# A gated recurrence on one core: the order of the twelve products of a step, and of one VectorE update

## The chip, the cores and the metric

The kernel runs on one core of a Trainium2 chip. The metric is the time of one execution on the device in microseconds (us), the median of several runs. A profile comes from one execution of its own. In it PE is TensorE (matmuls), PEld is TensorE's loading of the stationary operand, DVE is VectorE, ACT is ScalarE, POOL is GpSimd and SP is SyncE. L188 is line 188 of the kernel.

## The reference

x is (8 batches, 512 steps, 512 features), float32. Each step uses the state h of the step before:

```python
def step(h, x_t):
    fused = jax.nn.sigmoid(jnp.concatenate([x_t, h], axis=-1) @ w_W + w_b)
    hidden_state, output_state = jnp.split(fused, 2, axis=-1)
    memory_state = x_t @ wx_W + wx_b + hidden_state * (h @ wh_W + wh_b)
    h_new = output_state * h + (1.0 - output_state) * jnp.tanh(memory_state)
    return (h_new, h_new)
_, hs = jax.lax.scan(step, h0, xT)
return x + jnp.swapaxes(hs, 0, 1)
```

Below, r is the first half of the fused gate (hidden_state), z the second (output_state), and hh is h @ wh_W + wh_b. Every step needs three products of h (8 x 512) with 512 x 512 weights, for r, z and hh, and they can't start before the step before has given h. The products of x don't depend on h.

## The kernel before, in words

**Layout.** The 512 units of h are cut in four chunks k of 128. Chunks 0 and 1 are half A (`hT[0]`, in the profile hTA), chunks 2 and 3 half B (`hT[1]`, hTB). A chunk is the stationary operand of a product: 128 partitions x 32 columns, where the 32 columns are four steps x 8 batches, and only the columns of the present step are not zero. So the four steps of a group (`GS = 4`) add up in the same PSUM banks, and only the eight rows of the present step count (`rows`).

**Products.** The outputs are spread over the four 32-partition quadrants j of PSUM, so that each product consists of four matmuls of 32 output partitions, one in each column group of TensorE. There are three banks: A holds hh, z and r of half A (192 columns), B holds r and hh of half B (128 columns), C holds z of half B (64 columns). With four chunks each, a step has twelve products, A0 to A3, B0 to B3 and C0 to C3, each of four matmuls; a float32 matmul appears in the profile as two records. The order is written out by hand in `ORDER` (L27), and the first step has one of its own, `FIRST`. The loop at L338 issues them; the quadrant it begins with moves on:

```python
for j in range(NQ):
    j = (j + turn[0]) % NQ
    to = ps[bank] if i or bank != "A" else xps[0][:, XP["A"]]
    mm(to[32 * j : 32 * j + 32, :], hs, wh(bank, k, j))
```

Behind the twelve products of a step the loop takes seven quadrant matmuls of the x side (`take(later, 7)`, `turn[0] += 7`), 192 columns each, for a pair of groups that comes later (`products`). The x side ends some steps before the last one. Each bank exists twice; ScalarE copies the x side's part into the idle set in advance (`spread`).

**From the banks to the new h.** A product A0 needs chunk 0 of the new h, A1 chunk 1, A2 and A3 those of half B. The order of instructions on every engine is the order of the program. For each half (hf) VectorE transposes r (`turn_r`, L374, tr), hh (`turn_h`, L390, md1) and z (`turn_z`, L374, tz) out of PSUM; r and hh of half B come from bank B, its z from bank C. ScalarE takes the sigmoid of r (md0) and of z (hd0). `memory(hf, q)` is a scan on VectorE for chunk q of the half (L358, m) and a tanh of it on ScalarE. `update(hf, q)` is a scan on VectorE (L358, hTA or hTB) that makes the new h of the chunk, and the weight load of the next step's first product with that chunk waits for it. In the loop:

```python
turn_r(0)
turn_h(0)
turn_z(0)
memory(0, 0)
memory(0, 1)
turn_r(1)
turn_h(1)
update(0, 0)
turn_z(1)
tc.add_manual_dep(update(0, 1), r_done[1].name, SYNC)
```

and then memory(1, 0), memory(1, 1), update(1, 0) and update(1, 1). Behind these VectorE has one transposition of the x side (L256), in some steps an addition (L475) and two tiny memsets (L505); ScalarE copies the new h and prepares banks; GpSimd adds x to h for the output (L507), which SyncE's queue stores every 16 steps.

Of the kernel before, what the change touches and what calls it, by code (L numbers as in the profile page):

```python
# [23 lines left out]
LAST = 4  # L24
SYNC = mybir.DependencyInfo(mybir.DependencyClass.Sync, mybir.DependencyReason.DATA)

ORDER = "A0 B0 A1 A2 A3 B1 B2 B3 C0 C1 C2 C3"  # L27

FIRST = "A0 x A1 x A2 x A3 B0 B1 B2 B3 C0 C1 C2 C3"

# [11 lines left out]
def tile_cond_rnn_residual(  # L42
# [172 lines left out]
    def act(key, out_, in_, func, **kw):  # L215
        inst = nc.scalar.activation(out_, in_, func, **kw).ins  # L216
        if key in written:
            tc.declare_no_dep(inst, written[key], reason="ordered through VectorE")
        written[key] = inst
        return inst  # L220
# [108 lines left out]
    for i in range(T):  # L329
# [7 lines left out]

        for n in (ORDER if i else FIRST).split():  # L338
            if n == "x":
# [16 lines left out]
        def scan(c_, out_, d0, d1):  # L356

            return nc.vector.tensor_tensor_scan(  # L358
                *[t_[:, :, c_].rearrange("p n c s -> p (n c s)") for t_ in (out_, d0, d1)],
                0.0,  # L360
                ALU.mult,
                ALU.add,
            ).ins
# [8 lines left out]
        def turned(n, hf):  # L372
            t_ = work.tile([P, 2, 32], F32, tag=f"t{n}{hf}", name=f"t{n}{hf}_{i}")
            inst = nc.vector.transpose(t_.rearrange("p c n -> p (c n)"), raw[n][hf]).ins  # L374
            return t_[:, :, rows], inst
# [4 lines left out]
        def turn_r(hf):  # L380
            tr, _ = turned("r", hf)
            r_done[hf] = act(
                ("r", hf, g % 2, s),
                md0[hf][g % 2][:, rows, :, 1].rearrange("p n c -> p c n"),
                tr,
                AF.Sigmoid,
            )

        def turn_h(hf):
            inst = nc.vector.transpose(  # L390
                md1[hf][g % 2][:, :, :, 0].rearrange("p n c -> p c n"), raw["h"][hf]
            ).ins
            h_done[hf] = inst
            if hf == 0 and i + 1 - NH in pool_done:
                tc.add_manual_dep(inst, pool_done[i + 1 - NH].name, SYNC)

        def turn_z(hf):
            tz, _ = turned("z", hf)
            if hf == 0:
                inst = nc.vector.memset(idle[:, IDLE - 1 :], 0.0).ins  # L400
                tc.add_manual_dep(inst, h_done[0].name, SYNC)
            act(
                ("zc", hf, i % 2),
                hd0[hf][i % 2][:, :, :, 2].rearrange("p n c -> p c n"),
                tz,
                AF.Sigmoid,
                scale=-1.0,
            )
# [6 lines left out]
        def memory(hf, q):  # L415

            c_ = slice(q, q + 1)
            scan(c_, ms[hf], md0[hf][g % 2][:, rows], md1[hf][g % 2][:, rows])
            act(("n", hf, q, i % NH), state(hf, i, 1)[:, :, c_], ms[hf][:, :, c_, 1], AF.Tanh)

        def update(hf, q):
            s1 = (i + 1) % GS
            new = hT[hf][(i + 1) % NH][:, B * s1 : B * s1 + B]
            return scan(slice(q, q + 1), new, hd0[hf][i % 2], hT[hf][i % NH][:, rows])
# [4 lines left out]
        memory(0, 0)  # L429
        memory(0, 1)  # L430
        turn_r(1)
        turn_h(1)
        update(0, 0)
        turn_z(1)
        tc.add_manual_dep(update(0, 1), r_done[1].name, SYNC)
        if i == 0:
# [169 lines left out]
```

## Time and profile before

| | |
|---|---|
| median of 3 runs | 1672.12 us (1671.9 to 1674.32) |
| profiled execution | 1670.8 us, its span from the first to the last instruction |
| mean granted TensorE clock | 0.999 |
| busy: PE, PEld, DVE, ACT, POOL | 99%, 98%, 65%, 62%, 18% |
| matmul records: 192, 128, 64 columns | 329, 273, 219 ns (mean of one, with hTA) |

The profiled execution lies 1.3 us below the median of the runs. Each row of the page's groups gives the line, the engine, the operation, what it writes and reads, the shapes and the count; then the busy time of the group, the mean length of one, and the idle time of the engine just before them with what ended it. Matmuls are pipelined, several run at a time, and their ends are modelled, so a busy PE is not a PE at its peak. A row of a timeline gives the start, the length, the engine, the line, the operation and the count of records merged in it, and in brackets the idle time before it with what ended it.

### The profile page before, as it was taken

The numbers are of one execution on the slowest core, as the hardware profiler recorded it, in microseconds if no ns is written. First come the engines' busy times: TensorE is split into PE (matmuls) and PEld (weight loads), VectorE is DVE, ScalarE is ACT, GpSimd is POOL, SyncE is SP. The second block draws the span as 40 slices with busy tenths as digits, with TensorE's granted clock in tenths as the row PEclk, the third lists the DMA queues.
The fourth block names the chain that finished last, engine by engine and source line by source line (L and its number), as shares of the span: only waits on it lengthen the run. The fifth ranks groups of instructions, "written<-read, shape, count | busy, mean of one in ns | idle before, by whom it ended". The sixth has DMA issues, their size and how long they took to land.

```text
span 1670.8 us, 129875 instructions
## 1 busy us (share of the span) xinstructions
PE 1659.0 (99%) x56238; PEld 1637.5 (98%) x56238; DVE 1090.5 (65%) x9387; ACT 1029.9 (62%) x5822; POOL 301.9 (18%) x1281
## 2 busy tenths in 40 slices
PE   8999999999999999999999999999999999999998
PEld 5999999999999999999999999999999999999997
DVE  6666666666666666666666666666666666666666
ACT  3666666666666666666666666666666666666665
POOL 1111111111111111111111111111111111111111
PEclk9999999999999999999999999999999999999999
DMA  4000000000000000000000000000000000000000
GB/s 179 17 5 17 18 18 17 17 6 17 17 18 18 5 17 18 17 17 5 18 17 17 18 11 12 18 17 17 18 5 17 17 18 17 5 17 12 11 12 10
DMA packets 11525, 31.40 MB, mean 19 GB/s; under 512 B 1220, under 2 KB 1732, under 8 KB 10824
## 3 DMA queue, kind: packets, MB, share of 16 engines
q1 hardware_dynamic: 10800, 22.94, 4.0%
q8 instruction: 440, 7.21, 1.8%
q14 instruction: 133, 1.09, 0.2%
q10 hardware_dynamic: 152, 0.16, 0.0%
HBM read 14.70 MB, written 8.39 MB: 14 GB/s over the span
## 4 chain that ended last, share of the span: by engine, by line
PE 98%; DVE 1%; DMA 0%; issue 0%; ACT 0%
PE A L188 44%; PE B L188 23%; PE xp L188 20%; PE C L188 12%; DMA rows<-in_bias_dram 0%; DVE tr L374 0%; DVE m L358 0%; DVE tz L374 0%; DVE md1B L390 0%; DVE md1A L390 0%; DVE hTA L358 0%; DVE bias L203 0%; ACT hTB L216 0%; ACT xp L224 0%; DVE rows L120 0%
## 5 line engine op out<-in xcount | busy, mean ns | idle before, releaser
L188 PE MATMUL A<-wa,hTA 128*32 128x192 f32 x8176 | 638.2, 329 | 2.3 <-DVE hTA L358 2.3
L188 PE MATMUL B<-wb,hTA 128*32 128x128 f32 x8192 | 573.8, 273 | 0.0
L188 PE MATMUL A<-wa,hTB 128*32 128x192 f32 x8176 | 507.4, 326 | 0.5 <-DVE hTB L358 0.5
L188 PEld LDWEIGHTS B<-wb,hTA 128*32 128x32 f32 x8192 | 471.2, 122 | 1.4 <-issue 0.2
L374 DVE STREAM_TRANSPOSE tr<-A 128x64 f32<-128x64 f32 x511 | 127.7, 250 | 463.5 <-PE A L188 463.5
L188 PE MATMUL B<-wb,hTB 128*32 128x128 f32 x8192 | 398.9, 273 | 0.0
L188 PEld LDWEIGHTS A<-wa,hTA 128*32 128x32 f32 x8176 | 385.4, 123 | 7.6 <-DVE hTA L358 4.0
L188 PEld LDWEIGHTS A<-wa,hTB 128*32 128x32 f32 x8176 | 372.9, 122 | 2.7 <-DVE hTB L358 0.8
L216 ACT ACTIVATE md0A<-tr 128x16 f32<-128x16 f32 x512 | 112.3, 219 | 421.0 <-DVE tr L374 421.0
L507 POOL TENSOR_TENSOR ot<-xin,hTB 128x16 f32<-128x16 f32 x503 | 125.9, 250 | 1324.5 <-DVE hTB L358 1314.0
L188 PEld LDWEIGHTS B<-wb,hTB 128*32 128x32 f32 x8192 | 321.5, 122 | 0.1
L188 PE MATMUL C<-wb,hTA 128*32 128x64 f32 x8192 | 289.4, 219 | 0.0
L188 PE MATMUL C<-wb,hTB 128*32 128x64 f32 x8192 | 288.9, 220 | 0.2 <-issue 0.2
L188 PEld LDWEIGHTS C<-wb,hTA 128*32 128x32 f32 x8192 | 266.7, 122 | 0.0
L188 PE MATMUL xp<-tw,sx 128*32 128x192 f32 x2976 | 237.2, 326 | 0.1
L188 PEld LDWEIGHTS C<-wb,hTB 128*32 128x32 f32 x8192 | 229.2, 123 | 0.4 <-issue 0.4
L358 DVE TENSOR_TENSOR_SCAN hTB<-hd0B,hTB 128x24 f32<-128x24 f32 x1024 | 157.8, 195 | 101.0 <-ACT hTB L216 99.8
L358 DVE TENSOR_TENSOR_SCAN hTA<-hd0A,hTA 128x24 f32<-128x24 f32 x1024 | 191.0, 187 | 0.0
L188 PE MATMUL xp<-wx,xin 128*32 128x192 f32 (+1 forms) x2048 | 182.4, 331 | 0.7 <-issue 0.5
L216 ACT ACTIVATE hd0B<-tz 128x16 f32<-128x16 f32 x512 | 115.2, 225 | 93.7 <-DVE tz L374 93.7
L216 ACT ACTIVATE hTB<-hTB 128x16 f32<-128x16 f32 x512 | 120.5, 235 | 79.8 <-DVE hTB L358 72.3
L216 ACT ACTIVATE hTB<-m 128x8 f32<-128x8 f32 x1024 | 160.6, 206 | 0.0
(92 smaller groups left out, 2489.6 us busy)
## 6 DMA issues: line engine op xcount, KB each, us to landing
xin<-in_x_dram SPq DMA_DIRECT2D x31, 256.0 KB, 3.5
out_dram<-ot SPq DMA_DIRECT2D x31, 256.0 KB, 2.2
wx<-in_wx_dram SPq DMA_DIRECT2D x4, 768.0 KB, 7.1
wa<-in_wa_dram SPq DMA_DIRECT2D x4, 384.0 KB, 8.9
wb<-in_wb_dram SPq DMA_DIRECT2D x1, 1152.0 KB
wb<-in_wb_dram SPq DMA_DIRECT2D x1, 384.0 KB, 11.1
out_dram<-ot SPq DMA_DIRECT2D x1, 192.0 KB, 3.9
head<-in_xh_dram ACTq DMA_DIRECT2D x1, 144.0 KB, 5.0
```

The source lines that it names most:

```text
L188: nc.tensor.matmul(out_, lhsT, rhs, start=start, stop=False, skip_group_check=True)
L216: inst = nc.scalar.activation(out_, in_, func, **kw).ins
L358: return nc.vector.tensor_tensor_scan(*[t_[:, :, c_].rearrange("p n c s -> p (n c s)") for t_ in (out_, d0, d1)], 0.0, ALU.mult, ALU.add,).ins
L374: inst = nc.vector.transpose(t_.rearrange("p c n -> p (c n)"), raw[n][hf]).ins
L507: return engine.tensor_tensor(ot[:, t, 2 * hf : 2 * hf + 2, :].rearrange("p c n -> p n c"), x_of(c, slice(2 * hf, 2 * hf + 2), t, 1).rearr ...
```

## The change

The order of products is changed so that all four products of bank B (r and hh of half B) stand behind the four of bank A. On VectorE the first update of half A goes ahead of the transposition of hh of half B.

```diff
-ORDER = "A0 B0 A1 A2 A3 B1 B2 B3 C0 C1 C2 C3"
+ORDER = "A0 A1 A2 A3 B0 B1 B2 B3 C0 C1 C2 C3"
...
         memory(0, 0)
         memory(0, 1)
         turn_r(1)
+        update(0, 0)
         turn_h(1)
-        update(0, 0)
         turn_z(1)
         tc.add_manual_dep(update(0, 1), r_done[1].name, SYNC)
```

The first step keeps its own order of products.

## The prediction

> **What bounds the kernel now.** I read the page first, then the waits, then VectorE's, ScalarE's and TensorE's timelines of single steps in the middle of the run, and last the steps at its very end, which have no products of x.
>
> ```profile
> span 1670.8 us, 129875 instructions
> ...
> PE 1659.0 (99%) x56238; PEld 1637.5 (98%) x56238; DVE 1090.5 (65%) x9387; ACT 1029.9 (62%) x5822; POOL 301.9 (18%) x1281
> ...
> PEclk9999999999999999999999999999999999999999
> ...
> L188 PE MATMUL A<-wa,hTA 128*32 128x192 f32 x8176 | 638.2, 329 | 2.3 <-DVE hTA L358 2.3
> ...
> L188 PE MATMUL B<-wb,hTA 128*32 128x128 f32 x8192 | 573.8, 273 | 0.0
> ...
> L188 PE MATMUL C<-wb,hTA 128*32 128x64 f32 x8192 | 289.4, 219 | 0.0
> ...
> L216 ACT ACTIVATE hTB<-m 128x8 f32<-128x8 f32 x1024 | 160.6, 206 | 0.0
> ...
> PEld A L188 <- DVE hTA L358: 4.0, 11, 0.4
> ```
>
> TensorE looks full; the longest wait for h that it is charged with is 4.0 us in all (last row, from the waits). But a matmul of 273 or 329 ns is one of four that run side by side in the four column groups (the product's quadrant j), so a gap in one group is covered by the other three and appears in no idle column. I therefore take the time apart by group. The end of the run shows the groups in lockstep (TensorE's timeline; start, length, records):
>
> ```profile
> 1658.77 0.83 PE L188 MATMUL A<-wa,hTB 128*32 128x192 f32 x16
> 1659.42 0.40 PE L188 MATMUL B<-wb,hTA 128*32 128x128 f32 x8
> 1659.64 0.62 PE L188 MATMUL B<-wb,hTB 128*32 128x128 f32 x16
> 1660.08 0.41 PE L188 MATMUL C<-wb,hTA 128*32 128x64 f32 x16
> 1660.30 0.41 PE L188 MATMUL C<-wb,hTB 128*32 128x64 f32 x16
> ```
>
> A product is two records in each group. Sixteen A records are four per group: (1659.42 - 1658.77)/4 = 0.1625 us each. B: 24 records, six per group, (1660.08 - 1659.42)/6 = 0.11. C: (1660.30 - 1660.08)/4 = 0.055. A group owes each step eight of each kind: 8 x (0.1625 + 0.11 + 0.055) = 2.62 us. The x side adds seven quadrant products of 192 columns: three groups get 4 records (a long turn, 2.62 + 0.65 = 3.27), one gets 2 (a short turn, 2.62 + 0.325 = 2.945). The mean is 3.19. The start j rotates by seven, so the group that has just had its short turn is first in the next step's list: it leads, and it is the one that meets every wait.
>
> ```profile
> 73.58 0.25 DVE L374 STREAM_TRANSPOSE tr<-A 128x64 f32<-128x64 f32 x1 [0.94 <-PE A L188]
> 1618.98 0.25 DVE L374 STREAM_TRANSPOSE tr<-A 128x64 f32<-128x64 f32 x1 [0.95 <-PE A L188]
> 1631.82 0.25 DVE L374 STREAM_TRANSPOSE tr<-A 128x64 f32<-128x64 f32 x1 [0.73 <-PE A L188]
> 1656.59 0.25 DVE L374 STREAM_TRANSPOSE tr<-A 128x64 f32<-128x64 f32 x1 [0.94 <-PE A L188]
> 1659.67 0.25 DVE L374 STREAM_TRANSPOSE tr<-A 128x64 f32<-128x64 f32 x1 [0.94 <-PE A L188]
> ```
>
> Steps 16 to 496 take (1618.98 - 73.58)/480 = 3.220 us each, a few long ones included; the undisturbed four up to 1631.82 take 3.21. That is 0.02 above the 3.19 of pure streaming. Without x (last two rows) a step still takes 3.08: the loop of h through the other engines is nearly as long as the streaming. One step of that loop, on VectorE, with two tanh rows of ScalarE and two weight loads of TensorE:
>
> ```profile
> 802.27 0.25 DVE L374 STREAM_TRANSPOSE tr<-A 128x64 f32<-128x64 f32 x1 [1.02 <-PE A L188]
> 802.44 0.21 DVE L390 STREAM_TRANSPOSE md1A<-A 128x64 f32<-128x64 f32 x1
> 802.58 0.21 DVE L374 STREAM_TRANSPOSE tz<-A 128x64 f32<-128x64 f32 x1
> 802.81 0.28 DVE L358 TENSOR_TENSOR_SCAN m<-md0A,md1A 128x16 f32<-128x16 f32 x2
> 803.00 0.23 DVE L374 STREAM_TRANSPOSE tr<-B 128x64 f32<-128x64 f32 x1
> 803.15 0.21 DVE L390 STREAM_TRANSPOSE md1B<-B 128x64 f32<-128x64 f32 x1
> 803.28 0.20 DVE L358 TENSOR_TENSOR_SCAN hTA<-hd0A,hTA 128x24 f32<-128x24 f32 x1
> 803.40 0.22 DVE L374 STREAM_TRANSPOSE tz<-C 128x64 f32<-128x64 f32 x1
> 803.55 0.17 DVE L358 TENSOR_TENSOR_SCAN hTA<-hd0A,hTA 128x24 f32<-128x24 f32 x1
> 803.64 0.25 DVE L358 TENSOR_TENSOR_SCAN m<-md0B,md1B 128x16 f32<-128x16 f32 x2
> 804.09 0.31 DVE L358 TENSOR_TENSOR_SCAN hTB<-hd0B,hTB 128x24 f32<-128x24 f32 x2 [0.20 <-ACT hTB L216]
> ...
> 803.03 0.32 ACT L216 ACTIVATE hTA<-m 128x8 f32<-128x8 f32 x2
> ...
> 803.84 0.32 ACT L216 ACTIVATE hTB<-m 128x8 f32<-128x8 f32 x2
> ...
> 803.54 0.31 PEld L188 LDWEIGHTS A<-wa,hTA 128*32 128x32 f32 x8
> ...
> 804.35 0.36 PEld L188 LDWEIGHTS A<-wa,hTB 128*32 128x32 f32 x8
> ```
>
> Both first loads wait for VectorE: A0's comes at 803.54, 0.06 after the scan that ends at 803.48; A2's at 804.35, 0.06 after the first hTB scan (804.09 + 0.20, the length of the hTA scan of the same shape). Whether that wait costs anything depends on the leading group having other matmuls left. The step before shows both sides of that:
>
> ```profile
> 800.27 0.37 PE L188 MATMUL A<-wa,hTA 128*32 128x192 f32 x1
> ...
> 800.45 0.49 PE L188 MATMUL A<-wa,hTA 128*32 128x192 f32 x6
> 800.64 0.27 PE L188 MATMUL B<-wb,hTA 128*32 128x128 f32 x1
> 800.71 0.33 PE L188 MATMUL A<-wa,hTA 128*32 128x192 f32 x1
> ```
>
> The leader's late A0 record at 800.27 lasts 0.37 instead of 0.33: a matmul whose load came late pays 0.04 on top of the wait. And A0's eighth record starts at 800.71, after the leader's first B0 record at 800.64, which stands behind it in the program: groups run ahead of each other, and a late load holds its own group.
>
> **One formula.** The group that is last in step n issues the last matmul of each bank, has its short turn, and leads step n+1. If nothing holds it, 2.945 us lie between the same product of the two steps. If the loop from that product in step n, as the last group runs it, to h being loaded for it in step n+1 takes L, the group stalls d = L - 2.945. Each group leads once in four steps, so a step takes 3.19 + d/4 while only the leader stalls.
>
> Before, for A0. From A0's start the last group streams A0 0.325, B0 0.22, A1 to A3 0.975, of which the last record lasts 0.326 instead of 0.1625: 1.68. Then about 0.04 to VectorE (in the rows ahead the last A record of lockstep ends 1658.77 + 0.83 = 1659.60 and tr starts at 1659.67, 0.07, which I keep as the upper bound, with 0 as the lower; I take 0.04, with which this sum meets the measured step), 803.28 - 802.27 = 1.01 to the scan, its 0.20, 0.06 to the load, and the 0.04 of a late load: L = 3.03, d = 0.085, step 3.21. Measured: 3.21. For A2 in the same way: 0.65 of A2 and A3, again with the longer last record, 0.815; 0.04; 804.09 - 802.27 = 1.82; 0.20 + 0.06 + 0.04: 2.975, d = 0.03, less than the 0.085 that the leader has lost at A0 already. So before, the leader stalls at A0 and nowhere else.
>
> **The change part by part.** No instruction is added, and no DMA or queue entry of SP or POOL moves. Two things move.
>
> (1) B0 (eight records, two per group, 0.22 us) goes from between A0 and A1 to behind A3. Between A0 and the end of bank A there is 0.22 less, so A0's L falls to 2.81, below 2.945: A0's stall goes. That gives back 0.085/4 = 0.021 per step. VectorE's tr of half A follows bank A's end as before; but the ends of banks B and C now lie 0.22 later behind it. What each meets on VectorE:
> - tr<-B stands 0.73 behind tr<-A. Bank B's last record starts 0.1625 + 7 x 0.11 = 0.93 behind A's last, lasts 0.273 against 0.326: it ends 0.88 after A's end, and tr<-B now has to wait, some 0.15 us. Queued behind it are the second half's transposes and both updates of half A.
> - tz<-C stands 1.13 behind tr<-A. Bank C's last record starts 0.1625 + 8 x 0.11 + 7 x 0.055 = 1.43 behind A's last (eight B records, then eight of C), lasts 0.219: it ends 1.32 after A's. So tz<-C starts at about 1.32 and is 0.19 late; through B alone it would be 0.15 late. C decides. Behind it on VectorE stand update(0,1), both m scans and the hTB scans; ScalarE's sigmoid of it stands ahead of the two tanh.
>
> L for A2 is then: A2, A3 0.65, B 0.88, seven C records 0.385, the last 0.219, 2.13; 0.04 to VectorE; 804.09 - 803.40 = 0.69 from tz to the scan; 0.20 + 0.06 + 0.04: 3.16. d = 0.215, which costs 0.054 per step. By B alone it would be 0.65 + 0.77 + 0.273 + 0.04 + (804.09 - 803.00) + 0.30 = 3.12, d = 0.175, 0.044.
>
> (2) update(0,0) moves ahead of turn_h(1). The three items between tr<-B and tz<-C stay the same three, 803.40 - 803.00 = 0.40 in sum, so tz and what follows it do not move for it. The scan wants to start 0.15 behind tr<-B; its tanh, the first of the two at 803.03, ends at 803.24 by the 206 ns of the page's row, and the scan of before follows at 803.28. With tr<-B 0.15 late it starts at 803.30, so the wait of (1) just covers it. Without that cover it would wait for ScalarE about 0.13 and carry md1B and tz<-C with it. A0's h comes no later than now, and A0 isn't what is late. Worth: nothing.
>
> **Sum.** A step goes from 3.21 to 3.19 + 0.054, 3.244: +0.034. Products of x are issued in steps 5 to 500 (62 pairs of groups with 56 quadrant products each, seven a step), 496 of them: +16.9 us. The 11 steps without x go from 3.08 to 3.21 (the loop alone; for A0 above, L is 3.03 where these steps take 3.08, so I add 0.05 to 3.16): +0.13 each, +1.4. The profiled execution goes from 1670.8 to 1689.1; the median of the runs lies 1.3 above it: **1690.4**.
>
> Bounds: with 0.07 instead of 0.04 into VectorE d grows by 0.03, +3.7 us, 1694; with 0 it shrinks by 0.04, 1685. If C does not decide but B, 0.0225 x 496 + 1 = +12, 1684.
>
> **The rivals.**
> *All four groups held.* If the late load stops every group and not only the leader, the leader's lead is lost each step and the step is as long as a long turn, 3.27: +0.06 x 496 + 1.4 = +31, **1703**. Against it stand the rows of 800.27 to 800.71, where the groups run apart. For it: the leader of one step is the second group of the next, a long turn of 3.27 later against a step of 3.244, so with d = 0.215 the second group comes to A2 only 0.03 after the leader is let go, and a slightly longer L holds it too. The Trainium skill (TensorE: Matmul & The Clock Gate, Part 3, "The mechanism") says that matmuls start and end strictly in program order; that would be this rival, and the trace disagrees with it. Chance 0.14.
>
> *Faster: A0's stall goes and A2's does not come.* 0.021 x 496 = -10.4: **1662**. It needs L for A2 at 2.945 or less, 0.2 below my sum: tz<-C would have to start where it does now with C's end 0.22 later. For it speaks only that bank A really ends earlier after A0, and that the next load has cover to spare at A0. Against it, A2's load is already the one 0.06 behind its scan, and the change takes 0.22 of cover from in front of it. Chance 0.05.
>
> *Nothing that can be told.* The two stalls cancel (d at A2 about 0.085, L about 3.03): 1672. It needs 0.13 less than my sum, below the bound through B (3.12). Chance 0.05. A change of 0.2% (3.3 us) is about what a measurement of this kernel can tell from none.
>
> **How the numbers follow.** My case, 1682 to 1697, has 0.73; all groups held 0.14; 0.03 for something slower yet; faster 0.05; same 0.05. The range 1682 to 1704 takes in my bounds and the first rival. Slower by over 0.2%: 0.90.
>
> **What would show it.** Right: the idle time before VectorE's tr<-B, now none, is about 0.15 us a step and put down to PE B; tz<-C waits for PE C a few hundredths; the first hTB scan starts about 2.0 behind tr<-A instead of 1.82; A0's loads no longer sit directly behind their scan while the first A<-hTB record of a step comes late with the others' matmuls running on; the last steps are 3.2 apart. Wrong: tr<-B without a wait, first hTB scan still 1.82 behind tr<-A, or the end of the run at 3.08 or less; or steps of 3.27, with the four groups in lockstep in the middle of the run.

## The result, and the profile after

The changed kernel takes 1691.05 us (median of 4 runs, 1690.09 to 1692.14) against 1672.3 us of the kernel before in the same comparison: 1.011 of its time, 95% interval 1.0098 to 1.0122. The profiled execution went from 1670.8 to 1687.9 us. The forecast was 1690.4.

The page and the waits of the changed kernel:

```profile
span 1687.9 us, 129875 instructions
...
PE 1677.6 (99%) x56238; PEld 1607.4 (95%) x56238; DVE 1166.3 (69%) x9387; ACT 1071.6 (63%) x5822; POOL 301.1 (18%) x1281
...
L188 PE MATMUL A<-wa,hTA 128*32 128x192 f32 x8176 | 566.5, 326 | 0.2
L188 PE MATMUL A<-wa,hTB 128*32 128x192 f32 x8176 | 471.6, 329 | 0.9 <-DVE hTB L358 0.7
...
L188 PEld LDWEIGHTS A<-wa,hTB 128*32 128x32 f32 x8176 | 285.6, 123 | 50.4 <-DVE hTB L358 5.6
```

The same instructions, and TensorE as full as before. Two small things tell of the change: the mean A record with hTA went from 329 to 326 ns, the one with hTB from 326 to 329, so the matmuls that pay for a late load are now those of half B; and the weight loads of A<-hTB now have 50.4 us of idle time in front of them (2.7 before). The columns of waits still name next to nothing.

One step in the middle on VectorE, to be read beside the step from 802.27 to 805.46 in the prediction:

```profile
818.18 0.25 DVE L374 STREAM_TRANSPOSE tr<-A 128x64 f32<-128x64 f32 x1 [0.79 <-PE A L188]
...
818.71 0.28 DVE L358 TENSOR_TENSOR_SCAN m<-md0A,md1A 128x16 f32<-128x16 f32 x2
819.05 0.25 DVE L374 STREAM_TRANSPOSE tr<-B 128x64 f32<-128x64 f32 x1
819.23 0.17 DVE L358 TENSOR_TENSOR_SCAN hTA<-hd0A,hTA 128x24 f32<-128x24 f32 x1
819.31 0.22 DVE L390 STREAM_TRANSPOSE md1B<-B 128x64 f32<-128x64 f32 x1
819.50 0.25 DVE L374 STREAM_TRANSPOSE tz<-C 128x64 f32<-128x64 f32 x1
819.67 0.17 DVE L358 TENSOR_TENSOR_SCAN hTA<-hd0A,hTA 128x24 f32<-128x24 f32 x1
819.76 0.25 DVE L358 TENSOR_TENSOR_SCAN m<-md0B,md1B 128x16 f32<-128x16 f32 x2
820.20 0.31 DVE L358 TENSOR_TENSOR_SCAN hTB<-hd0B,hTB 128x24 f32<-128x24 f32 x2 [0.19 <-ACT hTB L216]
```

Counted from tr<-A, tr<-B comes at 0.87 (0.73 before), the first hTA scan at 1.05 (1.01), tz<-C at 1.32 (1.13), the first hTB scan at 2.02 (1.82). Half B's new h is 0.2 us later behind bank A's end. On TensorE in that step (matmuls, then weight loads), and last the weight load of A0 in the kernel before that belongs to the matmul of 800.27 in the prediction:

```profile
819.60 0.33 PE L188 MATMUL A<-wa,hTA 128*32 128x192 f32 x1
819.71 0.38 PE L188 MATMUL xp<-wx,xin 128*32 128x192 f32 x3
819.76 0.97 PE L188 MATMUL A<-wa,hTA 128*32 128x192 f32 x15
820.46 0.92 PE L188 MATMUL A<-wa,hTB 128*32 128x192 f32 x16
...
819.45 0.12 PEld L188 LDWEIGHTS A<-wa,hTA 128*32 128x32 f32 x1
...
820.46 0.56 PEld L188 LDWEIGHTS A<-wa,hTB 128*32 128x32 f32 x16
...
800.27 0.31 PEld L188 LDWEIGHTS A<-wa,hTA 128*32 128x32 f32 x7
```

A0's first load still comes directly behind its scan (819.23 + 0.17 = 819.40, the load at 819.45), but its matmul follows only at 819.60, at full pace (0.33 long), while before both began at 800.27 and the matmul took 0.37: the leader's earlier records now last longer than the wait for h, and the stall at A0 is gone. A2's first load comes at 820.46, 0.06 behind its scan (820.20 + 0.20), and its matmul starts with it. The leader's four A0 and A1 records had their turn from 819.60 to 820.25 (4 x 0.1625), so it stood still for about 0.2.

The records can be given to their column groups by the order of the program and the streaming times. In 275 of the 281 steps from 200 to 480 exactly one group comes late to A2; it loses 0.23 there on average, 0.19 of it waiting and 0.04 in its first record. A quarter of 0.23 on 3.19 gives 3.247, the measured step (3.246, below).

The three x records from 819.71 belong to the other groups and stand ahead of the A0 record of 819.60 in the program, so the groups still run apart. The Trainium skill (TensorE: Matmul & The Clock Gate, Part 3, "The mechanism") has matmuls start strictly in program order; these rows don't show that for matmuls in different column groups. They are records, though, and a float32 matmul has two: the first records of those x matmuls start at 819.54 to 819.60, so whole matmuls keep the program's order here. In the kernel before they don't: when the first C2 record starts, six records of C0 and C1 are still to start in 227 of the 280 steps from 200 to 479, and with whole matmuls in order it would be three at most.

How long a step is (tr<-A of steps 16, 496, 500, 503 and 511):

```profile
73.83 0.25 DVE L374 STREAM_TRANSPOSE tr<-A 128x64 f32<-128x64 f32 x1 [0.79 <-PE A L188]
...
1634.25 0.25 DVE L374 STREAM_TRANSPOSE tr<-A 128x64 f32<-128x64 f32 x1 [0.80 <-PE A L188]
...
1647.24 0.25 DVE L374 STREAM_TRANSPOSE tr<-A 128x64 f32<-128x64 f32 x1 [0.56 <-PE A L188]
...
1656.93 0.25 DVE L374 STREAM_TRANSPOSE tr<-A 128x64 f32<-128x64 f32 x1 [0.77 <-PE A L188]
...
1682.73 0.25 DVE L374 STREAM_TRANSPOSE tr<-A 128x64 f32<-128x64 f32 x1 [0.88 <-PE A L188]
```

Undisturbed, (1647.24 - 1634.25)/4 = 3.25 us (3.246 from the unrounded starts) against 3.210; without products of x, (1682.73 - 1656.93)/8 = 3.225 against 3.079. Over all of steps 16 to 496 the mean is (1634.25 - 73.83)/480 = 3.251 against 3.220: 0.031 x 496 + 0.146 x 11 = 17.0 us, and the profiled execution grew by 17.1.

### The profile page after: what moved, and what is told of

The parts are those of the page before. It is cut to its first block, busy times and chain, and to the rows that moved or that the text cites. A ratio compares the mean times of both kernels' runs of the same rounds, so it can differ in the third digit from the quotient of the medians.

```text
span 1687.9 us, 129875 instructions
## 1 busy us (share of the span) xinstructions
PE 1677.6 (99%) x56238; PEld 1607.4 (95%) x56238; DVE 1166.3 (69%) x9387; ACT 1071.6 (63%) x5822; POOL 301.1 (18%) x1281
## 4 chain that ended last, share of the span: by engine, by line
PE 98%; DMA 1%; DVE 0%; issue 0%; ACT 0%; SPq 0%
PE A L188 40%; PE B L188 26%; PE xp L188 19%; PE C L188 13%; DMA wb<-in_wb_dram 1%; DMA wx<-in_wx_dram 0%; ACT hTB L216 0%; ACT xp L224 0%; DVE hTB L358 0%; DVE tz L374 0%; SPq L125 0%; DVE tr L374 0%; DVE md1B L390 0%; DVE hTA L358 0%; ACT hd0B L216 0%
## 5 line engine op out<-in xcount | busy, mean ns | idle before, releaser
L188 PE MATMUL A<-wa,hTA 128*32 128x192 f32 x8176 | 566.5, 326 | 0.2
L188 PE MATMUL B<-wb,hTA 128*32 128x128 f32 x8192 | 343.1, 273 | 0.7 <-DMA wb<-in_wb_dram 0.7
L188 PE MATMUL B<-wb,hTB 128*32 128x128 f32 x8192 | 343.3, 273 | 0.1
L188 PEld LDWEIGHTS A<-wa,hTB 128*32 128x32 f32 x8176 | 285.6, 123 | 50.4 <-DVE hTB L358 5.6
L188 PEld LDWEIGHTS B<-wb,hTA 128*32 128x32 f32 x8192 | 292.6, 122 | 1.9 <-DMA wb<-in_wb_dram 1.1
L188 PEld LDWEIGHTS B<-wb,hTB 128*32 128x32 f32 x8192 | 265.7, 122 | 0.3 <-DMA wb<-in_wb_dram 0.3
L188 PE MATMUL C<-wb,hTB 128*32 128x64 f32 x8192 | 234.0, 219 | 0.4 <-issue 0.4
L188 PE MATMUL C<-wb,hTA 128*32 128x64 f32 x8192 | 234.0, 219 | 0.0
L188 PEld LDWEIGHTS C<-wb,hTA 128*32 128x32 f32 x8192 | 211.6, 122 | 0.0
L216 ACT ACTIVATE hTA<-m 128x8 f32<-128x8 f32 x1024 | 161.2, 207 | 0.0
```

The lines of the kernel that those rows point to most:

```text
L188: nc.tensor.matmul(out_, lhsT, rhs, start=start, stop=False, skip_group_check=True)
```

## The experiments

The theory is that of the prediction: a step costs 3.19 us of streaming plus a quarter of what the leading column group waits for h. That a step is never less than the loop of h itself is added here; the prediction's sum has it only for the steps without x. The rivals are that the moved update is at fault, that the order of products as such is (cover for another product, program order, streaming), and that every group, or none, pays for a late h. Times are compared with runs of the kernel before on the same chip, 1671.5 us for the first four experiments, 1672.7 for the next three, 1671.6 for the last two.

**The order of products alone.**

```diff
-ORDER = "A0 B0 A1 A2 A3 B1 B2 B3 C0 C1 C2 C3"
+ORDER = "A0 A1 A2 A3 B0 B1 B2 B3 C0 C1 C2 C3"
```

> The new order of products with the old order on VectorE. Theory (the leading column group stalls at A2 because banks B and C end later behind bank A; the move of the update is covered by the wait for bank B and worth nothing): as with the whole change, 1690 us within 3, the first hTB scan about 2.03 us behind tr<-A, the last steps 3.2 us apart. Rival (the moved update delays the transpose of hh of half B and is what costs): 1672 us, hTB scan at 1.82.

Measured: 1691.24 us, ratio 1.0115 (1.0101 to 1.0129). VectorE in one step, tr<-A at 820.18:

```profile
821.05 0.25 DVE L374 STREAM_TRANSPOSE tr<-B 128x64 f32<-128x64 f32 x1
821.22 0.23 DVE L390 STREAM_TRANSPOSE md1B<-B 128x64 f32<-128x64 f32 x1
821.35 0.17 DVE L358 TENSOR_TENSOR_SCAN hTA<-hd0A,hTA 128x24 f32<-128x24 f32 x1
821.50 0.25 DVE L374 STREAM_TRANSPOSE tz<-C 128x64 f32<-128x64 f32 x1
...
822.20 0.31 DVE L358 TENSOR_TENSOR_SCAN hTB<-hd0B,hTB 128x24 f32<-128x24 f32 x2 [0.19 <-ACT hTB L216]
```

tz<-C and the hTB scan lie where they lie in the whole change, 1.32 and 2.02 behind tr<-A, with the old order of the update. The first hTA scan stands at 1.17 instead of 1.05, so the moved update does give A0 its h 0.12 sooner; but nothing waits for it, since even here the first A0 matmul starts 0.05 behind its load (median of 280 steps). The order of products explains the whole loss; the update's move adds nothing to it. The rival of the update falls.

**The update alone.**

```diff
         turn_r(1)
+        update(0, 0)
         turn_h(1)
-        update(0, 0)
```

> The old order of products with update(0,0) in front of turn_h(1). Theory: tr<-B doesn't wait for bank B here, so the update stands behind its tanh for about 0.13 us and makes tz<-C about 0.10 late; L for A2 is 2.975 + 0.10 = 3.075, d = 0.13 instead of the 0.085 lost at A0, + 0.011 us a step: 1677 us, the hTA scan still 1.01 behind tr<-A. Rival 1 (the move gives A0 its h 0.13 earlier and is worth something): 1662 us. Rival 2 (the move is what costs in the whole change): 1691 us.

Measured: 1678.71 us, ratio 1.0041 (1.0028 to 1.0053). One step, tr<-A at 813.83:

```profile
814.56 0.22 DVE L374 STREAM_TRANSPOSE tr<-B 128x64 f32<-128x64 f32 x1
814.83 0.21 DVE L358 TENSOR_TENSOR_SCAN hTA<-hd0A,hTA 128x24 f32<-128x24 f32 x1
814.96 0.24 DVE L390 STREAM_TRANSPOSE md1B<-B 128x64 f32<-128x64 f32 x1
815.11 0.21 DVE L374 STREAM_TRANSPOSE tz<-C 128x64 f32<-128x64 f32 x1
```

The hTA scan stands at 1.00, no sooner than before: it waits for its tanh, and md1B and tz<-C wait with it on the engine that works in order. tz<-C is at 1.28 instead of 1.13, 0.15 late where I had expected 0.10: md1B follows the scan by 0.13. So the move is worth nothing with the new order and costs 0.4% with the old one. The cover that the prediction named for it, the wait for bank B, is real.

**B0 one place later, still ahead of A2.**

```diff
-ORDER = "A0 B0 A1 A2 A3 B1 B2 B3 C0 C1 C2 C3"
+ORDER = "A0 A1 B0 A2 A3 B1 B2 B3 C0 C1 C2 C3"
```

> B0 behind A1 instead of behind A0, everything else as before. Theory (what counts is that one B product stands in front of A2 as cover and one fewer behind A3; not where it stands ahead of A2): 1672 us, no change, step 3.21. Rival (B0 is cover for the second update of half A, so A1 directly behind A0 stalls): the load of A1 moves with its scan, the time lies between 1675 and 1691 us.

Measured: 1671.03 us, ratio 0.9998 (0.9989 to 1.0006). In the trace A1's first load moves from 1.75 to 1.50 behind tr<-A, to just behind its scan, and still costs nothing. What counts is on which side of A2 and A3 B0 stands.

**Two products of bank B ahead of A's end.**

```diff
-ORDER = "A0 B0 A1 A2 A3 B1 B2 B3 C0 C1 C2 C3"
+ORDER = "A0 B0 B1 A1 A2 A3 B2 B3 C0 C1 C2 C3"
```

> Two B products (B0 and B1) ahead of A's end, old VectorE order: the move in the other direction. Theory: L for A0 grows by the 0.22 us of B1 from 3.03 to 3.25, d = 0.305, 3.19 + d/4 = 3.266; but a step can't be shorter than the loop itself, 3.25 + 0.05 = 3.30 us, so all four groups are held: + 0.09 x 496 + 0.22 x 11 = 1719 us, and the last steps are 3.30 us apart like all the others. Rival 1 (only the leader ever stalls): + 0.056 x 496 + 2.4 = 1702 us. Rival 2 (the more of B stands in front of A2, the more cover, and the faster): 1655 us.

Measured: 1714.37 us, ratio 1.0258 (1.0242 to 1.0273). Steps 496, 500, 503 and 511 begin here:

```profile
1657.43 0.25 DVE L374 STREAM_TRANSPOSE tr<-A 128x64 f32<-128x64 f32 x1 [1.05 <-PE A L188]
...
1670.62 0.25 DVE L374 STREAM_TRANSPOSE tr<-A 128x64 f32<-128x64 f32 x1 [0.81 <-PE A L188]
...
1680.51 0.25 DVE L374 STREAM_TRANSPOSE tr<-A 128x64 f32<-128x64 f32 x1 [1.05 <-PE A L188]
...
1706.87 0.25 DVE L374 STREAM_TRANSPOSE tr<-A 128x64 f32<-128x64 f32 x1 [1.16 <-PE A L188]
```

(1670.62 - 1657.43)/4 = 3.298 us with products of x, (1706.87 - 1680.51)/8 = 3.295 without: the step is the loop, and the products of x come free. All four groups wait, by the records given to them: the leader 0.29 ahead of A0, and in each group the second A0 record comes 0.03 to 0.04 late. The expected 1719 was 5 us too much. More cover in front of A2 doesn't help; it lengthens the loop through bank A and A0.

**C0 in B0's old place, with the whole change.**

```diff
-ORDER = "A0 A1 A2 A3 B0 B1 B2 B3 C0 C1 C2 C3"
+ORDER = "A0 C0 A1 A2 A3 B0 B1 B2 B3 C1 C2 C3"
```

> The whole change, but with C0 where B0 stood: A0 C0 A1 A2 A3 B0 B1 B2 B3 C1 C2 C3. Bank C ends 0.055 x 2 = 0.11 us sooner behind bank A, bank B as late as in the whole change; A0's loop is 2.92, below 2.945. Theory (in the whole change C's end decides, and B's end lies close behind it): tz<-C starts 0.04 sooner behind tr<-A and no longer waits for the bank, L falls from 3.16 to the 3.12 of bank B, step about 3.233: 1684 us. Rival (C's end alone is what costs): L falls by the full 0.11 to 3.05, d = 0.105, 1675 us. Rival (B's end alone is what costs): 1691 us, no change against the whole change.

Measured: 1684.98 us, ratio 1.0072 (1.0058 to 1.0086). One step, tr<-A at 815.22:

```profile
816.09 0.25 DVE L374 STREAM_TRANSPOSE tr<-B 128x64 f32<-128x64 f32 x1
...
816.35 0.23 DVE L390 STREAM_TRANSPOSE md1B<-B 128x64 f32<-128x64 f32 x1
816.50 0.21 DVE L374 STREAM_TRANSPOSE tz<-C 128x64 f32<-128x64 f32 x1
...
817.19 0.31 DVE L358 TENSOR_TENSOR_SCAN hTB<-hd0B,hTB 128x24 f32<-128x24 f32 x2 [0.19 <-ACT hTB L216]
```

tr<-B still waits for bank B, 0.87 behind tr<-A; tz<-C follows md1B at once and comes at 1.28 instead of 1.32, the hTB scan at 1.97 instead of 2.02. So in the whole change bank C's end is what decides, bank B's lies close behind, as the prediction had it.

**h of half B later, no product moved: two tiny memsets.**

```diff
         turn_z(1)
+        for n in range(2):
+            nc.vector.memset(idle[:, n : n + 1], 0.0)
         tc.add_manual_dep(update(0, 1), r_done[1].name, SYNC)
```

> The kernel before with two memsets of one column on VectorE between turn_z(1) and update(0,1): the new h of half B comes about 0.15 us later in each step, and no product is moved. Theory (only the leading column group pays, and it leads once in four steps): L for A2 2.975 + 0.15 = 3.125, d = 0.18, step 3.235; with the end of the run 1685 us, and hTB scan at 1.96 behind tr<-A. Rival 1 (every step pays the delay in full): + 0.15 x 507 = 1747 us. Rival 2 (a step is the longer of streaming and loop, and the loop of 3.08 + 0.10 still lies below 3.21): 1672 us.

Measured: 1673.2 us, ratio 1.0 (0.9992 to 1.0009). The dose was not what I took it for. The trace has the hTB scan at 1.86 and not at 1.96 behind tr<-A: two memsets of one column delay what is behind them by 0.05 us, not by 0.15. (All these kernels have one such memset already, behind half A's tz, which the list of VectorE's work above leaves out.) With 0.05 the theory's L is 3.025, d = 0.08, below the 0.085 lost at A0: no cost. The run only excludes that each step pays in full (0.05 x 507 = 25 us); the time doesn't tell the theory from rival 2. The trace shows where the delay went: the first A2 matmul starts 0.105 behind its load in the kernel before and 0.055 here (medians of 280 steps in the middle of the run), so it ate half of the cover that was there.

**One such memset in the changed kernel.**

```diff
         turn_z(1)
+        nc.vector.memset(idle[:, :1], 0.0)
```

> The whole change with one such memset behind turn_z(1): h of half B about 0.06 us later. The changed kernel's last steps, the loop alone, take 3.225 us, its steps with products of x 3.246. Theory: the loop becomes 3.225 + 0.06 = 3.285, longer than 3.19 + d/4 = 3.26, so all four groups are now held and the step is the loop: + 0.04 x 496 + 0.06 x 11 = 1711 us, all steps 3.285 apart. Rival 1 (only the leader pays): + 0.015 x 496 + 1 = 1699 us. Rival 2 (each step pays in full already): + 0.06 x 507 = 1721 us.

Measured: 1702.7 us, ratio 1.018 (1.0166 to 1.0194). One step, tr<-A at 824.86:

```profile
826.18 0.25 DVE L374 STREAM_TRANSPOSE tz<-C 128x64 f32<-128x64 f32 x1
826.36 0.20 DVE L358 TENSOR_TENSOR_SCAN hTA<-hd0A,hTA 128x24 f32<-128x24 f32 x1
826.39 0.06 DVE L435 MEMSET idle<- 128x1 f32 x1
...
826.92 0.31 DVE L358 TENSOR_TENSOR_SCAN hTB<-hd0B,hTB 128x24 f32<-128x24 f32 x2 [0.19 <-ACT hTB L216]
```

The delay is 0.045 and not 0.06 (hTB scan at 2.06 behind tr<-A), so the loop is 3.27 and the time less than expected. Steps with and without x take the same 3.27 us, more than the leader's formula gives (3.26). But 3.27 is also the prediction's long turn, so this run doesn't show whether the loop or the streaming of the long turns sets the step, nor that all four groups are held: in this step the leader comes to A2 0.2 late (827.19) and the other three on time 0.04 to 0.06 behind it. Much the same delay that cost nothing in the kernel before costs 11.6 us here (1702.7 against 1691.1; the kernel before took 1672.7 and 1672.3 beside them).

**Longer memsets in the kernel before.** Since the small dose had missed, two larger ones, with a tile of 96 or 192 columns:

```diff
         turn_z(1)
+        nc.vector.memset(pad, 0.0)
```

> The kernel before with a memset of 96 columns on VectorE between turn_z(1) and update(0,1), no product moved: h of half B about 0.12 us later (the two memsets of one column made it 0.05 later, and 96 columns last some 0.08 longer). Theory, with the last steps T of each kernel as its loop: step = 3.19 + (T - 2.995)/4, as long as that is more than T. T = 3.08 + 0.12 - 0.07 (the delay that the two loops' difference hides) = 3.13, step 3.224: 1679 us. Rival 1 (a step is the longer of streaming, 3.21, and T): 1672 us. Rival 2 (each step pays the delay beyond 0.07 in full): + 0.05 x 507 = 1697 us.

> The same with a memset of 192 columns: h of half B about 0.20 us later, T = 3.08 + 0.20 - 0.07 = 3.21. Theory: step 3.19 + 0.215/4 = 3.244, + 0.033 x 496 + 0.13 x 11 = 1690 us, like the whole change although no product is moved. Rival 1 (a step is the longer of 3.21 and T): 1673 us. Rival 2 (in full beyond 0.07): + 0.13 x 507 = 1738 us. Rival 3 (the whole change is slow because of its order of products as such, not because h of half B comes late): 1672 us.

Measured: 1673.07 us with 96 columns, ratio 1.0007 (0.9998 to 1.0016), and 1685.21 with 192, ratio 1.0081 (1.0068 to 1.0095). The hTB scan came 0.08 and 0.18 later, where 0.12 and 0.20 were planned. The 96 columns alone can't be told from no change, and don't part the theory from rival 1. The 192 columns do: 1673 by rival 1, 1738 by rival 2, 1672 by rival 3, 1690 by the theory with the planned delay and, with the delay that came, T = 3.198 and 3.19 + 0.203/4 = 3.241: 0.031 x 496 + 0.12 x 11 = 17 us, where 13.6 were measured. The undisturbed step is the formula's (table below); the mean over steps 16 to 496 is 3.241 against 3.220, and single long steps make most of the difference: of these 480 steps, 13 are over 0.06 longer than the median in the profiled execution of the kernel before (3.2 us in sum), and 4 here (0.8). What makes single steps long was not tried. A late h of half B alone, with the old order of products, makes most of the whole change's loss. One step (line numbers are one higher here, tr<-A at 815.47; the hTB scan stands at 1.99):

```profile
816.60 0.23 DVE L375 STREAM_TRANSPOSE tz<-C 128x64 f32<-128x64 f32 x1
816.82 0.22 DVE L436 MEMSET pad<- 128x192 f32 x1
816.96 0.14 DVE L359 TENSOR_TENSOR_SCAN hTA<-hd0A,hTA 128x24 f32<-128x24 f32 x1
...
817.46 0.31 DVE L359 TENSOR_TENSOR_SCAN hTB<-hd0B,hTB 128x24 f32<-128x24 f32 x2 [0.20 <-ACT hTB L217]
```

**All kernels together.** T is the mean of the last eight steps, the loop alone; the step is the mean of the four steps 496 to 499, with products of x, both from the unrounded starts of tr<-A in each trace. The formula, put down before the last two ran, is 3.19 + (T - 2.995)/4, or T if that is more; 2.995 is the 2.945 of a short turn and the 0.05 that the prediction added for the loop alone, which it had from the kernel before.

| kernel | T | formula | step |
|---|---|---|---|
| before | 3.079 | 3.211 | 3.210 |
| B0 behind A1 | 3.079 | 3.211 | 3.210 |
| two memsets | 3.080 | 3.211 | 3.213 |
| memset of 96 columns | 3.098 | 3.216 | 3.216 |
| update alone | 3.139 | 3.226 | 3.227 |
| C0 in place | 3.182 | 3.237 | 3.235 |
| memset of 192 columns | 3.198 | 3.241 | 3.240 |
| order alone | 3.224 | 3.247 | 3.248 |
| the whole change | 3.225 | 3.247 | 3.246 |
| the change and a memset | 3.270 | 3.270 | 3.272 |
| two B products ahead | 3.296 | 3.296 | 3.298 |

Whatever made the loop longer, an order of products or an instruction of VectorE, the step follows T with a quarter of its growth up to about 3.25, and in the last two rows it is T within 0.002. Of these two only the last lies clear of the long turn of 3.27. The quarter also shows without T: by the records given to the groups, the leader's stall is 0.23 with the order alone, 0.19 with C0 in place and 0.21 with the 192 columns (0.09 at A0 and 0.12 at A2); a quarter of it on 3.19 is the measured step within 0.003. None of these kernels is faster than the kernel before.

## Why the prediction was right, point by point

**What bounds the kernel.** Streaming of 3.19 us in each group, and a loop that reaches only the group that leads: the table and the leader's stalls bear out both, and the quarter. The 0.04 into VectorE was chosen so that the sum meets the step before, and that agreement is no test; but the trace of the kernel before has 0.037 from the end of bank A's last record to tr<-A (median of 280 steps in the middle of the run).

**The two stalls.** A0's is gone and A2's has come, as the matmuls at 819.60 and 820.46 show. From the steps, d at A2 is 4 x (3.246 - 3.19) = 0.22, from the groups' records 0.23 (sum: 0.215).

**Banks B and C on VectorE.** tr<-B 0.14 late (0.15), tz<-C at 1.32 (1.32), C deciding with B close behind: seen in the trace and in the run with C0 in place. The hTB scan, at "about 2.0", came at 2.02.

**The update.** Worth nothing under the cover of the wait for bank B, 0.4% without it: both shown.

**Sizes that were off.** The last steps take 3.225, not 3.21: from tz<-C to the hTB scan it is now 0.70 instead of 0.69; the rest, some 0.005, lies in the surcharge of 0.05, which was taken from A0's loop, and in rounding. The undisturbed step grew by 0.036 instead of 0.034 (the formula's own two terms, 0.054 - 0.021, give 0.033; 0.034 came from the rounded 3.21). The long steps that I had left alone cost less in the changed kernel (mean 3.251 against 3.246 undisturbed, before 3.220 against 3.210), so the sum over 496 steps came out at 15.4 instead of 16.9 us. So the profiled execution came out 1.2 us below the sum's 1689.1; that the median still lies 0.7 above the forecast is because it lies 3.1 above the profiled execution here, not 1.3. How close the median came is therefore partly luck: two misses of 1.2 and 1.8 us with opposite signs.

**Signs that failed.** A0's loads were to sit no longer directly behind their scan; they still do (819.45), and only the matmul behind the load shows that nothing waits. I had also written that 0.15 us of idle time before tr<-B, put down to PE B, would show. The waits name this only once:

```profile
DVE tr L374 <- PE B L188: 1.3, 1, 1.3
```

The row before tr<-B, the m scans, begins at 818.71 and lasts 0.28: only 0.06 of idle time is left of a delay of 0.14, because two VectorE instructions in a row overlap by some 0.08 where nothing holds them. Starts have to be compared, not idle time. The same holds for tz<-C behind md1B.

**The rivals.** All groups held: not here, but with two B products ahead, and a loop 0.045 us longer (the change with a memset) already makes steps of its 3.27. It was as near as the 0.03 of the prediction said. The prediction took matmuls in program order for this rival; that was a slip, since the leader's A2 is also the first A2 in the program, and what the other groups still have to do at that time stands ahead of it. Faster, and no change: A2's L did not come near 2.945 or 3.03.

## What to carry to other kernels

Where several column groups of TensorE run side by side and one leads, a page that shows 99% busy and no waits can still hide a loop of dependences that costs a fraction of every step; a stretch of the same run in which the bulk work has ended shows the loop's own length, and how near it is. A product that looks like filler between two dependent ones is cover on one side and delay on the other: add up the loop for each wait that it stands in, and put it where the longest of them is shortest. Moving an instruction ahead on an engine that works in order helps only if its input is there; else it takes what is behind it along.

## What the runs showed of the hardware that was not expected

On VectorE, rows of short instructions overlap, so a short one costs what follows less than its own length. One memset of one column (a row of 0.06 us) between a transposition and a scan delayed what is behind it by 0.045 us in the changed kernel, and two of them by 0.05 in the kernel before. A memset of 96 float32 columns delayed it by 0.08 and one of 192 columns by 0.18, about 1 ns for each column from 96 to 192. A transposition that had to wait for its bank takes 0.25 us, and the next instruction follows it by 0.17; without a wait it is 0.23 and 0.15 (tr<-B and md1B with the order alone and in the kernel before).
